# Pacing the input statistics and giving TensorE idle transposes at the start of a two-layer graph-attention and mixture-of-experts kernel

## The chip, the cores and the metric

One NeuronCore of one Trainium2 chip runs the whole program in one launch. The metric is the device time of one execution in microseconds (us), the median of several runs. Five engines work beside each other, each through its own instructions in program order: TensorE (PE; its weight loads are listed apart as PEld), VectorE (DVE), ScalarE (ACT), GpSimd (POOL) and SyncE (SP, here the queue that issues most DMAs). They wait for each other on semaphores.

## The reference, cut to what matters

The input `x` is 2708 x 256 in float32, `adj` is 2708 x 2708 in int32. Each of two layers is a graph attention followed by a top-2 mixture of experts. The change touches only the first steps of the first attention:

```python
def _layernorm(x, axis=-1, eps=1e-5):
    m = jnp.mean(x, axis=axis, keepdims=True)
    v = jnp.var(x, axis=axis, keepdims=True)
    return (x - m) / jnp.sqrt(v + eps)

def _L0_gnn_ref(x, adj, W, a):
    h = x @ W.T
    a1, a2 = (a[:F_OUT], a[F_OUT:])
    s_i = h @ a1
    s_j = h @ a2
    e = jax.nn.leaky_relu(s_i[:, None] + s_j[None, :], negative_slope=0.2)
    att = jnp.where(adj > 0, e, NEG_INF)
    att = jax.nn.softmax(att, axis=1)
    return att @ h

x = x + _L0_gnn_ref(_layernorm(x, axis=-1), adj, L0_gnn_W, L0_gnn_a)
x = x + _L0_ffn_ref((_layernorm(x, axis=-1))[None], ...)[0]
x = x + _L1_gnn_ref(_layernorm(x, axis=-1), adj, 1, L1_gnn_W_gcn, L1_gnn_W_att, L1_gnn_a_att)
x = x + _L1_ffn_ref((_layernorm(x, axis=-1))[None], ...)[0]
```

## The kernel before

The 2708 rows of `x` are held in 22 tiles: 20 of 128 rows and two of 74. The stages follow each other: the front (normalise, project and score all 22 tiles), the attention of layer 0 in 11 pairs of tiles, the experts of layer 0, the attention of layer 1, its experts. The order of instructions on PE, ACT, DVE and SP is the order in which the program writes them.

**Before the front.** SP issues the loads of `x`, of the weight `L0_gnn_W` (two 128 KB pieces), of the score vectors `a0`, of the first two tiles of `adj`, and some fills of a scratch buffer. POOL builds the 128 x 128 identity `ident`. PE then transposes the weight: four transposes into the tile `w0_ps` (L341), which ACT copies to `w0_t` (L344). `score_weights` has DVE multiply `w0_t` with `a0` (L351).

**The front loop** (from L1438) counts steps 0, 1, 2, ...; step `t` begins tile `t`. At the head of each step DVE takes the statistics of some more tiles (`read_tile`: `bn_stats` at L481 and `bn_aggr` at L482). Up to and including step `s` it has read `min(T, 2 + 2 * step)` tiles: two for each step, all 22 by step 10. The tiles are read in groups, the list `firsts`: two pairs (0, 1), (2, 3), then groups of four. When the last tile of a group is read, `deviations(group)` is started: in that step ACT computes the reciprocal deviation in two activations (`root`, L488 and L489), and one step later DVE mends it by one Newton step of three small instructions (`mend`, L391).

The rest of a step is handed out by `Turns`, a list of generators. Every entry that is due is moved one stage on, older entries first. A tile's own generator is `front(t, r)`:

- step t: DVE normalises the tile into `xn` (L497), with four buffers; POOL adds it to the running sum `x_total` (L1254);
- step t+1: PE transposes it in two halves into `tr_ps` (L515);
- step t+2: ACT copies the result to `xt` (L1259);
- step t+3: PE projects it with `w0_t` in four matmuls into `h_ps` (L520; two calls, each seen as two records);
- step t+4: ACT writes `g_all` (L1264, L1265);
- for odd t: PE spreads the scores of the pair into `e_ps` at step t+5 (L1287), and DVE copies them to `e_bc` (L1291) at step t+6.

Among these lie the masks of the first two tiles of `adj`. DVE turns a first part of the integer rows to 8-bit masks (L1316), a step later PE transposes them (`mask_turn`, L1302, into a PSUM tile with the tag `mt`, of which there are two), another step later ACT copies them away (L1308). Tile 0 has its two DVE parts in steps 9 and 12, tile 1 in steps 14 and 17. After a tile's second DVE part SP issues the load of the tile of `adj` two further on.

At step `START` = 21 the attention begins: ACT and DVE build the weights `z` of one pair of tiles against tile `j` (L1332, L1335), and four steps later PE accumulates them (`gather`, L1346, `att_ps`). After tile 21 `front_mean` closes the front: PE multiplies `x_total` (L1273), and the result goes into the last row block of `g_all`.

Of the kernel before, what the change touches and what calls it, by code (L numbers as in the profile page):

```python
# [22 lines left out]
P = 128  # L23
# [124 lines left out]
def kernel(  # L148
# [25 lines left out]
    nc = tc.nc  # L174
# [7 lines left out]
    T = TF + 2  # L182
# [3 lines left out]
    tiles = [(t, P if t < TF else TAIL) for t in range(T)]  # L186
    pairs = [tiles[k:k + 2] for k in range(0, T, 2)]
    chunks = [tiles[k:k + 4] for k in range(0, T, 4)]
    firsts = [tiles[0:2], tiles[2:4]] + chunks[1:]

    ENDS1, EARLY_ENDS1 = (6, 12, 18, T), (12, 18)
    groups1 = [tiles[a:b] for a, b in zip((0, *ENDS1), ENDS1)]
# [25 lines left out]
    def ps_tile(name, tag="wide", dtype=F32):  # L218
        return stage["pool"].tile([P, 2048 // mybir.dt.size(dtype)], dtype, name=name, tag=tag,
                                  bufs=stage["tags"][tag])  # L220
# [95 lines left out]
    ident = const.tile([P, P], F32, name="ident")  # L316
# [17 lines left out]
    def w0_tile():  # L334
        return keep0.tile([P, DC * (D + 3)], F32, name="w0_t")

    w0_t = w0_tile().rearrange("p (c d) -> p c d", c=DC)
    for c in range(DC):
        ps = ps_tile("w0_ps")
        for o in range(DC):  # L340
            nc.tensor.transpose(  # L341
                ps[:, o * P:(o + 1) * P], w0_rows[o][:, c * P:(c + 1) * P], ident
            )
        nc.scalar.copy(w0_t[:, c, :D], ps[:, :D])  # L344

    def score_weights():
        raw = a0_pool.tile([P, DC, 2], F32, name="raw")
        for c in range(DC):
            for k in range(2):
                junk = row_tile("junk", 4)  # L350
                nc.vector.scalar_tensor_tensor(  # L351
                    junk, w0_t[:, c, :D], 1.0, a0[k], op0=OP.mult, op1=OP.mult,
                    accum_out=raw[:, c, k:k + 1])
        for k, (which, coef) in enumerate(((1, 0.2), (1, 0.8), (0, 0.8))):
            nc.scalar.activation(w0_t[:, :, D + k], raw[:, :, which], AF.Copy, scale=coef)
# [205 lines left out]
    def sums_d(name, zero=False):  # L561

        t = dram.tile([W + P, D], F32, name=name)
        lo = 0 if zero else T
        nc.sync.dma_start(t[lo * P:, :].rearrange("(t p) d -> p t d", p=P),
                          nobody[:, :D].unsqueeze(1).to_broadcast([P, T + 1 - lo, D]))
        return t
# [196 lines left out]
    def parts_of(name, b2):  # L764
        E = b2.shape[0]
        whole = [xn_tile()[:, :D] for _ in range(2)]
        part = [xt_tile()[:, :P].bitcast(BF16) for _ in range(3)]
        nc.gpsimd.memset(whole[0], 0.0)
        for k in range(3):
            nc.gpsimd.dma_start(whole[0][32 * k:32 * k + E], b2)  # L770
        for k in range(3):
            a = whole[k % 2]
            nc.gpsimd.tensor_copy(part[k], a)
            if k < 2:
                nc.gpsimd.tensor_tensor(whole[1 - k % 2], a, part[k], OP.subtract)
        res = const.tile([P, D], BF16, name=name)
        for k in range(3):
            nc.gpsimd.tensor_copy(res[32 * k:32 * k + 32], part[k][32 * k:32 * k + 32])
        return res
# [16 lines left out]
    class Experts:  # L796
# [163 lines left out]
        def weigh(self, b):  # L960

            xg = self.rows[b]
            side, w = (self.pool.tile([P, 1], F32, name=nm, bufs=3) for nm in ("side", "w"))
            nc.vector.tensor_scalar(side, xg[:, D + 1:D + 2], mine_of[:, b:b + 1], -0.5,  # L964
                                    op0=OP.is_equal, op1=OP.add)
            nc.scalar.activation(w, xg[:, D + 2:D + 3], AF.Tanh, scale=side)  # L966
            return w
# [282 lines left out]
    def front(t, r):  # L1250

        xn = xn_tile()[:, :D]
        ln_a0.apply(xn[:r], x_all[:r, t, :], t, r)
        nc.gpsimd.tensor_tensor(x_total[:r], x_total[:r], xn[:r], OP.add)  # L1254
        yield 1
        ps = turn_rows(xn[:r], r)
        yield 1
        xt = xt_tile().rearrange("p (c n) -> p c n", n=P)
        nc.scalar.copy(xt[:, :, :r], ps)  # L1259
        yield 1  # L1260
        ps = ps_tile("h_ps", "acc")
        project(ps[:r, :D + 3], xt, w0_t, r)
        yield 1 if t < LAST else 2
        nc.scalar.activation(g_all[:r, t, D:], ps[:r, D:D + 3], AF.Exp)  # L1264
        nc.scalar.activation(g_all[:r, t, :D], ps[:r, :D], AF.Copy, scale=g_all[:r, t, D:D + 1])  # L1265
        if t % 2:
            yield 1
            yield from front_spread(pairs[t // 2])

    def front_mean():  # L1270
        ps = ps_tile("total_ps", "acc")[:, :DC * 96].rearrange("p (c n) -> p c n", n=96)
        for c in range(DC):
            nc.tensor.matmul(ps[:, c], x_total[:, c * P:(c + 1) * P], ones_f, start=True, stop=True)  # L1273
        total = row_tile("junk", 4)[:, :DC * 96].rearrange("p (c n) -> p c n", n=96)
        yield 1
        nc.scalar.copy(total, ps)
        yield 1
        mean = ps_tile("mean_ps", "acc")
        project(mean[:96, :D], total, w0_t[:, :, :D], 96)
        yield 1  # L1280
        nc.scalar.activation(g_all[64:96, LAST, :D], mean[64:96, :D], AF.Copy, scale=TINY / N)
# [30 lines left out]
    def mask_tile(i, r, first, turn, keep):  # L1312

        for part, (lo, hi) in enumerate(PARTS):
            cols = slice(2 * P * lo, min(2 * P * hi, N))
            nc.vector.tensor_scalar(mask_rows(i)[:r, cols], adj_rows(i)[:r, cols], 0.0, -1.0,  # L1316
                                    op0=OP.is_gt, op1=OP.mult, saturate=False)
            if part and i + 2 < T:
                load_adj(*tiles[i + 2])
            yield first  # L1320
            mask_turn(i, r, part)
            yield keep
            mask_keep(i, r, part)
            if not part:
                yield max(turn - keep - first, 0)
# [14 lines left out]
    def gather(pair, j):  # L1340
        k = rows_of(j)
        z = zs.pop((pair[0][0], j))
        for q, (i, r) in enumerate(pair):
            if j == 0:
                accs[i] = ps_tile("att_ps", "acc")
            nc.tensor.matmul(accs[i][:r, :D + 1], z[:k, q * P:q * P + r], g_all[:k, j, :D + 1],  # L1346
                             start=(j == 0), stop=(j == LAST))
# [74 lines left out]
    late, read = [], 0  # L1422

    def read_tile():

        group = next(g for g in firsts if g[0][0] <= read <= g[-1][0])
        ln_a0.stats(x_all[:group[read - group[0][0]][1], read, :], *group[read - group[0][0]])
        if read == group[-1][0]:
            turns.start(deviations(group))
# [8 lines left out]
    for step in range(START + T * len(pairs)):  # L1438
        for _ in range(fills.get(step, 0)):
            router0.fill(filled_to, filled_to + 10)  # L1440
            filled_to += 10
        while read < min(T, 2 + 2 * step):
            read_tile()
            read += 1
        if step == 0:
            turns.step()
            score_weights()
        if step < T:
            turns.start(front(*tiles[step]))
        if step == T:  # L1450
            turns.start(front_mean())
        if step == START:
            sums0 += [sums_d(f"sums0_{k}", zero=k == 1) for k in range(2)]
        if step >= START:
            k, j = divmod(step - START, T)
            weigh(pairs[k], j)
            late.append((pairs[k], j))
            if len(late) > LAG:
                gather(*late.pop(0))
            if j == LAG - 1 and k > 0:  # L1460
                turns.start(close0(pairs[k - 1], LAG, 3), 3)
            if k + 1 < len(pairs) and j in (0, 11):
                nxt = pairs[k + 1]
                if j // 11 < len(nxt):
                    turns.start(mask_tile(*nxt[j // 11], 4, 4, 3))
            if (k, j) == (2, 0):
                experts0.load_b1()
            if j == 8 and k in (1, 2):
                b2_parts.append(parts_of(f"b2_{k - 1}", (L0_ffn_b2, L1_ffn_b2)[k - 1]))
            if k == len(pairs) - 1 and j == 16:  # L1470
                assert experts0.known
                experts0.fetch(0)
                for b in range(2):
                    experts0.load(b)
                    experts0.fetch(b + 1)
        turns.step()
# [1025 lines left out]
```

## Time and profile before

| what | value |
|---|---|
| median of 3 runs | 1133.14 us (1131.94 to 1135.37) |
| the profiled execution: time | 1137.78 us |
| the profiled execution: span of its instructions | 1136.1 us |
| PE busy over the span | 1039.2 us (91%) |
| DVE busy over the span | 545.7 us (48%) |
| first normalised tile (`xn` of tile 0) begins | 9.03 us |
| first transpose of tile 0, of tile 21 (L515) | 9.59 us, 45.65 us |
| first accumulation of the attention (L1346) | 49.95 us |
| the load of `adj` tile 2 is issued; its mask is begun | 31.89 us; 44.67 us |

The profile is one execution. A busy PE is modelled to the end of its pipelined matmuls. Timeline lines give the start and the duration in us, the engine, the line of the kernel, the operation, output<-inputs, shapes and a count; a bracket gives the idle time before the instruction and what ended it. Consecutive instructions of one line are merged into one row with a count. A window line gives busy time and instruction count for each engine in a stretch, then the granted TensorE clock (1.00 is full) and the DMA share.

### The profile page before, as it was taken

How to read it: one execution, taken by the hardware profiler on the slowest of the kernel's cores; microseconds unless marked ns; L12 is line 12 of the kernel's file. 1: busy time of each engine (PE TensorE's matmuls, PEld its weight loads, DVE VectorE, ACT ScalarE, POOL GpSimd, SP SyncE). 2: the span in 40 equal slices, each digit the busy share in tenths (PEclk: the TensorE clock that was granted, in tenths of full speed). 3: DMA queues.
4: the chain of work that ended last, by engine and by line, in shares of the span. 5: the costliest groups of instructions: out<-in, count | busy, mean ns of one | idle time of the engine just before them, and what ended most of it. 6: DMA issues, size and time to landing. Idle time of an engine off the chain costs nothing. (4 is left out here: it accounts for less than half of the span.)

```text
span 1136.1 us, 21474 instructions
## 1 busy us (share of the span) xinstructions
PE 1039.2 (91%) x6707; PEld 922.6 (81%) x6707; DVE 545.7 (48%) x2210; ACT 577.9 (51%) x1602; POOL 368.7 (32%) x425
## 2 busy tenths in 40 slices
PE   5999999998989999999999999898994957999984
PEld 3888888887879999999999954898983846999873
DVE  7788888886431110011001347578775643122257
ACT  4876767665434444444444446445653522444454
POOL 7531113111242211222123271352623155443350
PEclk9999999999989999999999999999997878999998
DMA  9955444431888999999899959301215645685893
GB/s 295 313 211 174 139 175 149 172 94 36 306 256 279 324 325 319 319 325 314 257 311 366 338 156 296 133 1 56 76 39 150 163 145 129 154 208 100 227 315 110
DMA packets 161862, 234.38 MB, mean 206 GB/s; under 512 B 10891, under 2 KB 137798, under 8 KB 159032
## 3 DMA queue, kind: packets, MB, share of 16 engines
q1 hardware_dynamic: 143356, 209.90, 56.0%
q0 software_dynamic: 18384, 23.03, 10.6%
q8 instruction: 56, 0.92, 0.3%
q14 instruction: 66, 0.54, 0.1%
HBM read 205.54 MB, written 54.59 MB: 229 GB/s over the span
## 5 line engine op out<-in xcount | busy, mean ns | idle before, releaser
L996 DVE TENSOR_SCALAR yo<-out_ps,w 128x256 f32<-128x256 f32 x89 | 43.1, 484 | 384.0 <-PE out_ps L990 376.7
L1346 PE MATMUL att_ps<-g_all,z 128*128 128x257 f32 (+3 forms) x968 | 225.3, 385 | 0.0
L1346 PEld LDWEIGHTS att_ps<-g_all,z 128*128 128x128 f32 (+3 forms) x968 | 176.0, 187 | 29.9 <-issue 2.9
L990 PE MATMUL out_ps<-room,ht 128*128 128x256 f32 x840 | 192.0, 381 | 0.0
L972 PEld LDWEIGHTS hid_ps<-xt,room 128*128 128x128 f32 x1504 | 175.8, 193 | 9.6 <-issue 5.0
L972 PE MATMUL hid_ps<-xt,room 128*128 128x128 f32 x1504 | 177.8, 276 | 5.8 <-issue 2.6
L990 PEld LDWEIGHTS out_ps<-room,ht 128*128 128x128 f32 x840 | 155.9, 191 | 20.2
L1332 ACT ACTIVATE zr<-e_bc,minus_one,g_all 128x256 f32<-128x256 f32 (+3 forms) x242 | 130.5, 591 | 41.8 <-DVE z L1335 41.5
L1773 PE MATMUL att_ps<-half,wide_mask 128*128 128x258 f32 (+1 forms) x962 | 130.6, 295 | 14.2 <-issue 7.2
L976 ACT ACTIVATE ht<-hid_ps,w_t 128x128 f32<-128x128 f32 x376 | 128.7, 364 | 28.2 <-PE hid_ps L972 8.3
L1001 POOL DMA_INDIRECT sums<-yo,xg x43 | 66.8, 1554 | 226.9 <-DVE side L964 152.8
L1773 PEld LDWEIGHTS att_ps<-half,wide_mask 128*128 128x128 f32 (+1 forms) x962 | 124.5, 199 | 17.6 <-issue 13.3
L753 POOL DMA_INDIRECT rows_d<-xr,place x88 | 91.7, 1041 | 119.8 <-DVE xr L497 66.5
L1335 DVE SCALAR_TENSOR_TENSOR z<-zr,mask_t 128x256 f32<-128x256 f32 (+3 forms) x242 | 99.1, 428 | 35.1 <-ACT zr L1332 19.1
L976 ACT ACTIVATE ht<-hid_ps,w1x 128x128 f32<-128x128 f32 x180 | 65.0, 366 | 82.5 <-PE hid_ps L972 68.1
L1001 POOL DMA_INDIRECT sums<-yo,xr x42 | 65.3, 1554 | 122.9 <-DMA sums<-yo,xr 34.5
L966 ACT ACTIVATE w<-xg,side 128x1 f32<-128x1 f32 x43 | 12.7, 294 | 163.4 <-DVE side L964 159.5
L1621 POOL CAST wide_mask<-mask_t 128x1408 fp32r<-128x1408 fp8e4 x34 | 47.0, 1388 | 93.1 <-PE att_ps L1773 92.9
L515 PE MATMUL tr_ps<-ident,xr 128*128 128x128 f32 (+1 forms) x214 | 39.3, 294 | 15.3 <-ACT xr L506 13.0
L972 PE MATMUL hid_ps<-lo,wide_mask 128*128 128x128 f32 x368 | 49.5, 290 | 3.5 <-ACT lo L1108 2.9
L972 PEld LDWEIGHTS hid_ps<-lo,wide_mask 128*128 128x128 f32 x368 | 47.9, 205 | 5.7 <-ACT lo L1108 3.9
L515 PEld LDWEIGHTS tr_ps<-ident,xr 128*128 128x128 f32 (+1 forms) x214 | 27.8, 152 | 22.9 <-ACT xr L506 14.3
(334 smaller groups left out, 1450.4 us busy)
## 6 DMA issues: line engine op xcount, KB each, us to landing
room<-in_L_ffn_W_dram SPq DMA_DIRECT2D x94, 1024.0 KB
room<-in_adj_dram SPq DMA_DIRECT2D x20, 1354.0 KB
wide_mask<-in_L_ffn_w_dram SPq DMA_DIRECT2D x46, 512.0 KB
room<-in_L_ffn_w_dram SPq DMA_DIRECT2D x22, 512.0 KB
mask_t<-in_L_ffn_w_dram SPq DMA_DIRECT2D x22, 512.0 KB
rows_d<-nobody SPq DMA_DIRECT2D x1, 7511.0 KB
rows_d<-nobody SPq DMA_DIRECT2D x5, 1295.0 KB
sums<-nobody SPq DMA_DIRECT2D x2, 2944.0 KB
```

Of the source, the lines that this page charges most:

```text
L515: nc.tensor.transpose(ps[:, c, :r], src[:, c * P:(c + 1) * P], ident[:r, :r])
L753: ins = nc.gpsimd.indirect_dma_start(out=self.rows_d[:, :], in_=self.rows[t][:r], in_offset=None, out_offset=bass.IndirectOffsetOnAxis(ap= ...
L972: nc.tensor.matmul(ps[:, :P], w1_b[:, c, f * P:(f + 1) * P], xt[:, c, :], start=(c == 0), stop=(c == DC - 1))
L976: nc.scalar.activation(ht[:, f, :], ps[:, :P], self.func, bias=self.bias[:, f, b:b + 1])
L990: nc.tensor.matmul(ps[:, :D], ht[:, f, :], self.rooms[b % self.deep][1][:, f, :], start=False, stop=(f == self.FC - 1))
L996: nc.vector.tensor_scalar(yo, ps[:, :D], w, None, op0=OP.mult)
L1001: ins = nc.gpsimd.indirect_dma_start(out=self.sums[k][:, :], in_=yo, in_offset=None, out_offset=bass.IndirectOffsetOnAxis(ap=self.rows.pop ...
L1332: nc.scalar.activation(zr[:k, :n], e_bc[:k, lo:lo + n], AF.Relu, bias=minus_one[:k], scale=g_all[:k, j, D + 1:D + 2])
L1335: nc.vector.scalar_tensor_tensor(z[:k, :n], zr[:k, :n], 1.0, mask_t[:k, j // 2, lo:lo + n, j % 2], op0=OP.add, op1=OP.mult)
L1346: nc.tensor.matmul(accs[i][:r, :D + 1], z[:k, q * P:q * P + r], g_all[:k, j, :D + 1], start=(j == 0), stop=(j == LAST))
L1621: nc.gpsimd.tensor_copy(m, src)
L1773: nc.tensor.matmul(accs[i][:, :D + 2], last_masks[i][:k] if late else wide_masks[i, j % 2][:k, j // 2, :], half_k[:k, j, :], start=(j == 0 ...
```

## The change

Three edits. The groups of the statistics become four pairs for the first eight tiles (before: two pairs and one group of four). The statistics are read at a slower pace from step 4 on: by step `s` there have been `2 + 2s - max(s - 2, 0) // 2` tiles, so that steps 4, 6, 8, 10, 12 and 13 read one tile and steps 5, 7, 9 and 11 read two; the last is read in step 13. And PE transposes the identity into a PSUM tile that nobody reads, six times ahead of the transposes of the weight and six times behind them.

```diff
-    firsts = [tiles[0:2], tiles[2:4]] + chunks[1:]
+    firsts = [tiles[k:k + 2] for k in range(0, 8, 2)] + chunks[2:]
...
+    def keep_busy(n):
+
+        ps = ps_tile("busy_ps", "mt")
+        for _ in range(n):
+            nc.tensor.transpose(ps[:, :P], ident, ident)
+
     w0_t = w0_tile().rearrange("p (c d) -> p c d", c=DC)
+    keep_busy(6)
     for c in range(DC):
         ps = ps_tile("w0_ps")
         for o in range(DC):
...
         nc.scalar.copy(w0_t[:, c, :D], ps[:, :D])
+    keep_busy(6)
...
-        while read < min(T, 2 + 2 * step):
+        while read < min(T, 2 + 2 * step - max(step - 2, 0) // 2):
             read_tile()
             read += 1
```

## The prediction

> **What bounds the kernel now.** I read first the stretches of the span, to find which engine is full where; then the timeline of 0 to 50 us engine by engine, since the change ends at step 13; then who waited for whom between 4 and 32 us. The chain that ended last covers only the end of the program and says nothing of the front.
>
> Busy time by stretch (PE, PEld, DVE, ACT, POOL; then clock, DMA share, GB/s):
>
> ```profile
> 10.00:15.00 5.00, 4.20 (x13) 3.08 (x12) 4.69 (x19) 2.05 (x8) 4.78 (x30) 1.00 1.15 316
> 25.00:30.00 5.00, 3.55 (x17) 2.56 (x16) 4.80 (x18) 2.42 (x8) 1.73 (x3) 0.73 1.09 309
> 35.00:40.00 5.00, 5.00 (x38) 4.37 (x37) 3.84 (x8) 4.09 (x14) 3.96 (x6) 1.00 0.98 340
> 100.00:150.00 50.00, 50.00 (x299) 43.62 (x298) 43.60 (x160) 33.33 (x69) 11.73 (x14) 1.00 0.48 169
> ```
>
> Until 30 us DVE is full and PE has holes; from 35 us PE is full and DVE is not; in the attention PE never pauses. So a microsecond won before the first accumulation moves all that follows by a microsecond, as long as nothing later is tied to absolute time, and I find no such thing.
>
> What fills DVE is seen in one step, step 8:
>
> ```profile
> 23.24 0.42 DVE L481 BATCH_NORM_STATS2 bn<-h_all 128x6 f32<-128x256 f32 x1
> 23.69 0.18 DVE L482 BATCH_NORM_AGGREGATE mv_a<-bn 128x2 f32<-128x6 f32 x1
> 23.79 0.39 DVE L481 BATCH_NORM_STATS2 bn<-h_all 128x6 f32<-128x256 f32 x1
> 24.22 0.18 DVE L482 BATCH_NORM_AGGREGATE mv_a<-bn 128x2 f32<-128x6 f32 x1
> 24.32 0.13 DVE L391 SCALAR_TENSOR_TENSOR stat<-mv_a,rstd_a 128x4 f32<-128x4 f32 x1
> 24.48 0.16 DVE L391 SCALAR_TENSOR_TENSOR stat<-stat,rstd_a 128x4 f32<-128x4 f32 x1
> 24.68 0.16 DVE L391 SCALAR_TENSOR_TENSOR rstd_a<-stat,rstd_a 128x4 f32<-128x4 f32 x1
> 24.76 0.41 DVE L497 TENSOR_SCALAR xn<-h_all,mv_a,rstd_a 128x256 f32<-128x256 f32 x1
> ```
>
> Two statistics take 1.08 us from start to start (23.24 to 24.32), one 0.54; a mend 0.44; only the last row feeds PE in this step. The waits say the same: PE's transposes waited 4.7 us for it.
>
> ```profile
> PE tr_ps L515 <- DVE xn L497: 4.7, 4, 2.8
> ```
>
> Two more things act on the front. POOL's running sum and DVE hold each other up:
>
> ```profile
> 15.18 0.73 POOL L1254 TENSOR_TENSOR x_total<-x_total,xn 128x256 f32<-128x256 f32 x1
> 15.32 0.60 DVE L391 SCALAR_TENSOR_TENSOR stat<-mv_a,rstd_a 128x4 f32<-128x4 f32 x1
> ```
>
> The mend of 0.13 us took 0.60 and ended when POOL did (15.92 against 15.91). Statistics in the same place keep their 0.39 to 0.43. And TensorE's clock is half at two times:
>
> ```profile
> 13.71 1.94 PE L520 MATMUL h_ps<-w_t,xt 128*128 128x259 f32 x4
> ...
> 18.70 1.04 PE L520 MATMUL h_ps<-w_t,xt 128*128 128x259 f32 x4
> ...
> 28.11 1.93 PE L520 MATMUL h_ps<-w_t,xt 128*128 128x259 f32 x4
> ```
>
> The same four matmuls take 1.94 us, then 1.04, then 1.93. The granted clock reads 0.50 from 28 to 30 us, after the hole of 1.43 us in which PE waited for the first mask. Before 17 us it reads 1.00 although the durations are doubled, so there I go by the durations.
>
> **The change, part by part.** Nothing is removed but the order.
>
> *The twelve transposes.* Four cold ones in the trace (L341) come as 0.45 us for the first and 0.90 us for three, so about 0.22 us each behind the first. Six take 0.45 + 5 x 0.22 = 1.55 us. The identity is ready at 1.62 us and the weight lands at 4.50, so the first six end by 3.2 and cost nothing; the second six run from about 6.7 to 8.2, and tile 0 wants PE at 9.59. Without that cover they would cost 2 x 1.55 = 3.1 us. Nobody reads their PSUM tile; the two `mt` buffers are next wanted by PE itself, in step 10. What do they bring? At best a full clock from 9.6 to 17 us. Tiles 4 and later wait for DVE, however: the transpose of tile 4 at 18.23 begins 0.74 us after PE was free, on `xn`. A quicker PE before that gains nothing by itself; I take 0, with 0.5 us for the upper end.
>
> Here the Trainium skill, "TensorE: Matmul & The Clock Gate", Part 4 (PE-mode transpose), speaks against the edit: transposes, it says, don't count as PE activity for the clock. Part 1 asks for some 3.4 us of sustained work. By that rule the clock is as cold at 9.6 us as before and the edit is worth 0; were it wrong, DVE makes it 0 all the same. This case's rows don't decide it: PE was all but continuously busy from 11.05 us with transposes and matmuls mixed, and was warm only near 17.
>
> *One more group.* Four pairs for a pair, a pair and a four: one more root (0.30 + 0.20 us on ACT) and one more mend (0.44 us on DVE). ACT is busy 2.05 of 5 us there and covers its part; behind the new root, which waits for tile 5's statistics at 11.97, stands the copy of tile 1, now at about 12.5; PE wants it at 13.7. DVE's 0.44 is paid in full.
>
> *The pace.* No instruction fewer: 22 statistics as before, but by `xn` of tile 9 three fewer are ahead of it. All of them come back in steps 10 to 13 (1, 2, 1, 1 where there were 2, 0, 0, 0), among the masks of tile 0. I follow DVE from tile 5, with statistics 0.54 each, mend 0.45, `e_bc` 0.33, mask parts 0.85 and 0.68 (all start to start), `xn` 0.32 to the next start and 0.41 to its end. POOL's sum runs 0.72 us from 0.14 after each `xn`; a DVE operation other than statistics or `e_bc` that meets it ends behind it (mend at once, `xn` 0.15 later, as at 32.86 to 33.62 in the trace). Until 18 us I leave all as it was: step 4 saves one statistic, but its mend then meets POOL's sum at 15.2 just as it did. End of `xn`:
>
> - tile 6: 19.54 + 0.54, held by POOL, 20.64 (before 21.48)
> - tile 7: 20.55 + 1.08 + 0.33 + 0.45 + 0.41 = 22.82 (23.33)
> - tile 8: 22.73 + 0.54, held, 23.83 (25.17)
> - tile 9: 23.74 + 1.08 + 0.85 + 0.33 + 0.41 = 26.41 (27.75)
> - tile 10: 26.32 + 0.54, mend held to 27.65, + 0.41 = 28.06 (29.59)
> - tile 11: 27.97 + 1.08 + 0.33 + 0.41 = 29.79 (31.19)
> - tile 12: 29.70 + 0.54, mask held to 31.3, mend, 32.08 (32.60)
> - tile 13: 32.00 + 0.54 + 0.33 + 0.41 = 33.28 (33.62)
> - tile 14: 33.19 + 0.85, mend held to 35.2, 35.6 (35.23)
>
> The lead is 1.3 to 1.5 us at tiles 8 to 11 and is given back by tile 14, which is even 0.4 late: the statistics were deferred, not saved. But PE had not used DVE's old lead there: it transposed tile 14 at 36.90, 1.67 us after `xn`. Now it can at 35.75, 1.15 us earlier; ACT's copy of a mask part and of tile 12 (34.9) take some 0.15 of it. From then on PE is full again at 1.32 us for a tile (29.83 to 45.65, twelve tiles), DVE's lead of 1.3 us for tile 15 on suffices, and the gain of **1.0 us** stays. On SP the load of `adj` tile 2 stands behind mask part two of tile 0: 31.3 + 0.7, hardly moved from 31.89, with 12 us until its mask.
>
> Bounds: below, if every deferred statistic ends in a POOL hold, -0.9 us (the mend twice over). Above, PE alone: from tile 4 at 18.23, 17 tiles at 1.32 would put tile 21 at 40.7 for 45.65, 5.0 us. I stand near the lower of these because the DVE rows between 10 and 35 us leave only 1.3 us idle in 25.
>
> **Sum.** 1136.1 - 1.0 = 1135.1 us of span; the profiled time lies 1.7 above its span and 4.6 above the median, so the same 1.0 from the median: 1133.14 - 1.0 = **1132.1 us**, with 1131.0 to 1133.2 if this case holds.
>
> **The rivals.**
>
> 1. *Nothing is gained*: DVE's sum of work to tile 14 is the same plus 0.44, and ACT's in-order copies behind roots that now come in steps 11 and 13 eat the rest. For it: DVE 4.8 of 5 us. Against it: PE's unused lead of 1.67 us at tile 14. 1133.14 + 0.2 = 1133.3 us.
> 2. *Much is gained*: with other timings DVE's mend and `xn` of tile 4 slip between POOL's sums at 15 to 18 us (they were held 0.45 + 0.6 + 0.63 = 1.7 us), and the hole before the first mask no longer cools PE (3.4 us at half, 1.7 us of work). 1.0 + 1.7 + 1.7 = 4.4: 1128.7 us. Against it: both holds depend on tenths, and the hole stays about 1.1 to 1.4 us by my rows.
> 3. *Slower*: PE now waits for the mask's second part and the late `xn` in steps 12 to 14 and falls to half clock there. Two such stretches of 3.4 us cost 1.7 us each beside the 0.9 of the lower bound: 4.3, 1137.4 us. It decides from the point where PE's holes in 31 to 37 us reach the 1.43 that cooled it at 27. Against it: I find holes under 1 us.
>
> **How the numbers follow.** Forecast 0.52, rival 1 0.22, rival 2 0.18, rival 3 0.08. About 0.3% (3.4 us) is what a measurement of this kernel tells from no change; the three runs shown spread by as much. Faster by more takes nearly all of rival 2: 0.17. Slower by more takes most of rival 3: 0.07. The rest, 0.76, lies within. The range reaches to rival 2's edge and past rival 1: 1128.9 to 1135.2.
>
> **What would show it.** Right: `xn` of tile 9 ends near 26.4, of tile 14 near 35.6; tile 21 is transposed near 44.6 and the first accumulation begins near 48.9; four projections still take about 1.9 us at 13 us; DVE rows of L391 and L497 beside POOL's L1254 are still stretched. Wrong: the projections take 1.04 us from the start and tile 4 is transposed before 17.5 (the transposes count after all, and PE was worth more than I say), or the first accumulation moves by over 2 us either way, or it moves as I say and the attention behind it doesn't follow.

## The result, and the profile after

Twelve runs of each kernel were made beside each other. Before: median 1133.47 us (1130.48 to 1136.45). Changed: 1134.55 us (1129.45 to 1137.37). The ratio on record is 0.9998 with a 95% interval of 0.998 to 1.0016 (the two medians by themselves give 1.0010): no difference that these runs can tell, and none above some 2 us either way. The profiled execution of the changed kernel has a span of 1134.3 us, against 1136.1.

The front did become shorter, in the two profiles by twice what was predicted. In the profile of the changed kernel (timeline of PE; start, duration):

```profile
12.07 2.07 PE L528 MATMUL h_ps<-w_t,xt 128*128 128x259 f32 x4
...
17.55 0.41 PE L523 MATMUL tr_ps<-ident,xn 128*128 128x128 f32 x2 [0.21 <-DVE xn L505]
...
24.99 0.51 PE L1310 MATMUL mt_ps<-ident_bf,room 128*128 128x128 bf16 x6 [1.35 <-DVE room L1324]
...
25.55 1.04 PE L528 MATMUL h_ps<-w_t,xt 128*128 128x259 f32 x4
...
43.56 0.29 PE L523 MATMUL tr_ps<-ident,xn 74*128 74x74 f32 x2
...
47.87 1.03 PE L1354 MATMUL att_ps<-g_all,z 128*128 128x257 f32 x4
```

(Lines of the changed kernel from the edit on stand 7 or 8 further down: L523 for L515, L1354 for L1346.) The projections still begin at half clock. Tile 4 is transposed at 17.55 for 18.23, tile 21 at 43.56 for 45.65, and the attention's first accumulation begins at 47.87 for 49.95: 2.08 us earlier. By its last accumulation the lead is 1.1 us (294.7 for 295.8). The stretches that answer to those shown before:

```profile
10.00:15.00 5.00, 4.05 (x12) 2.91 (x13) 4.62 (x22) 1.84 (x8) 4.78 (x30) 1.00 1.15 317
25.00:30.00 5.00, 4.42 (x28) 3.41 (x28) 4.80 (x17) 3.30 (x11) 2.19 (x3) 1.00 1.10 269
35.00:40.00 5.00, 5.00 (x34) 4.32 (x33) 4.75 (x9) 4.50 (x15) 4.17 (x6) 1.00 1.04 309
100.00:150.00 50.00, 50.00 (x298) 43.71 (x295) 42.84 (x158) 34.43 (x71) 12.59 (x15) 1.00 0.47 162
```

From 25 to 30 us PE does more (4.42 for 3.55) at a full clock. DVE is as full as before there, and from 35 to 40 us it is fuller, 4.75 for 3.84: the deferred work has moved. The attention is unchanged.

What is new stands between 50 and 80 us (timeline, DVE's masks and PE's use of the last):

```profile
57.90 0.99 DVE L1324 TENSOR_SCALAR room<-room 128x1536 fp8e4<-128x1536 int32 x1 [3.82 <-DMA room<-in_adj_dram]
...
69.34 0.96 DVE L1324 TENSOR_SCALAR room<-room 128x1536 fp8e4<-128x1536 int32 x1 [4.04 <-DMA room<-in_adj_dram]
...
70.36 0.51 PE L1310 MATMUL mt_ps<-ident_bf,room 128*128 128x128 bf16 x6 [0.71 <-DVE room L1324]
```

DVE waits for the loads of `adj` tiles 3 and 4, 7.9 us together (0.4 before), and PE stops for the second, for 0.71 us. That is one place where the lead goes. The next sections ask how much of the lead each edit makes, where it is given back, and why the total doesn't show it.

### The profile page after: what moved, and what is told of

Same layout as the page of the kernel before. It is cut to its first block, busy times and chain, and to the rows that moved or that the text cites. A ratio compares the mean times of both kernels' runs of the same rounds, so it can differ in the third digit from the quotient of the medians.

```text
span 1134.3 us, 21500 instructions
## 1 busy us (share of the span) xinstructions
PE 1045.1 (92%) x6719; PEld 927.5 (82%) x6719; DVE 541.2 (48%) x2213; ACT 577.6 (51%) x1604; POOL 366.3 (32%) x425
## 5 line engine op out<-in xcount | busy, mean ns | idle before, releaser
L1354 PE MATMUL att_ps<-g_all,z 128*128 128x257 f32 (+3 forms) x968 | 225.4, 385 | 0.0
L1354 PEld LDWEIGHTS att_ps<-g_all,z 128*128 128x128 f32 (+3 forms) x968 | 175.9, 187 | 29.8 <-issue 2.9
L1340 ACT ACTIVATE zr<-e_bc,minus_one,g_all 128x256 f32<-128x256 f32 (+3 forms) x242 | 130.2, 591 | 46.2 <-DVE z L1343 45.9
L1781 PE MATMUL att_ps<-half,wide_mask 128*128 128x258 f32 (+1 forms) x962 | 134.0, 299 | 14.5 <-issue 6.9
L1781 PEld LDWEIGHTS att_ps<-half,wide_mask 128*128 128x128 f32 (+1 forms) x962 | 127.3, 202 | 18.4 <-issue 14.0
L1343 DVE SCALAR_TENSOR_TENSOR z<-zr,mask_t 128x256 f32<-128x256 f32 (+3 forms) x242 | 96.0, 416 | 31.9 <-ACT zr L1340 18.7
L523 PE MATMUL tr_ps<-ident,xr 128*128 128x128 f32 (+1 forms) x214 | 39.7, 297 | 14.8 <-ACT xr L514 13.0
L523 PEld LDWEIGHTS tr_ps<-ident,xr 128*128 128x128 f32 (+1 forms) x214 | 28.1, 153 | 22.6 <-ACT xr L514 14.3
```

The costliest lines, as they stand in the source:

```text
L523: nc.tensor.transpose(ps[:, c, :r], src[:, c * P:(c + 1) * P], ident[:r, :r])
L1340: nc.scalar.activation(zr[:k, :n], e_bc[:k, lo:lo + n], AF.Relu, bias=minus_one[:k], scale=g_all[:k, j, D + 1:D + 2])
L1343: nc.vector.scalar_tensor_tensor(z[:k, :n], zr[:k, :n], 1.0, mask_t[:k, j // 2, lo:lo + n, j % 2], op0=OP.add, op1=OP.mult)
L1781: nc.tensor.matmul(accs[i][:, :D + 2], last_masks[i][:k] if late else wide_masks[i, j % 2][:k, j // 2, :], half_k[:k, j, :], start=(j == 0 ...
```

## The experiments

Totals differ between chips: `before_again`, `after_again`, `stats_only` and `busy_only` were made where the kernel before takes 1102 us, `pace_only`, `pairs_only`, `busy_24t` and `busy_12m` where it takes 1134, the last four of the table where it takes 1138. Each has one profile. So runs are compared by marks in their own profiles: when PE begins the first and the last accumulation of layer 0's attention (L1346 in the numbering before), how long DVE waited there for `adj` (47 to 110 us), and whether TensorE's clock fell once between 250 and 270 us. "Between" is the difference of the two marks.

| run | first | last | between | DVE for adj | clock fall |
|---|---|---|---|---|---|
| before | 49.95 | 295.8 | 245.8 | 0.4 | yes |
| before_again | 49.21 | 293.4 | 244.2 | 0.9 | no |
| busy_only | 49.76 | 295.6 | 245.9 | 1.1 | yes |
| pairs_only | 48.63 | 292.8 | 244.2 | 5.4 | no |
| pace_only | 47.84 | 293.9 | 246.1 | 7.4 | yes |
| stats_only | 47.79 | 293.7 | 245.9 | 1.9 | yes |
| changed kernel | 47.87 | 294.7 | 246.8 | 7.9 | yes |
| after_again | 47.85 | 293.7 | 245.9 | 4.3 | yes |
| busy_24t | 47.82 | 294.9 | 247.1 | 7.8 | yes |
| busy_12m | 47.73 | 292.9 | 245.1 | 7.9 | no |
| after_zero_late | 47.82 | 293.4 | 245.6 | 2.2 | yes |
| after_fills_late | 48.73 | 294.5 | 245.8 | none | yes |
| after_nosum | 46.71 | 294.2 | 247.5 | 8.5 | yes |
| before_nosum | 46.95 | 293.4 | 246.5 | 5.1 | yes |

**Both kernels once more**, unchanged.

> The kernel before, unchanged, once more. If the front is set by DVE's order, the first accumulation of the attention begins again near 49.95 us (within 0.3) and the attention's last accumulation near 295.8. If the clock's phase sets it, it moves by 0.5 us or more, with the time at which the four projections fall from 1.9 to 1.04 us. The total may differ by several us, through the second layer.

> The changed kernel, unchanged, once more. DVE's order: first accumulation again near 47.9 us, last one near 294.7, with DVE waiting for adj's load at about 58 and 69 us as in the first profile. If the wait for adj was chance, it is gone and the last accumulation is near 293.7.

The changed kernel repeats to 0.02 us on another chip. The kernel before does not: 49.21, 0.74 us earlier. In the two profiles `xn` of tiles 2 to 18 ends within 0.04 us, so DVE didn't make the difference; PE's rows part at 27 us, over the clock. In the second profile PE isn't cooled by the hole before the first mask. Its projection there (timeline of PE, before_again):

```profile
27.71 1.04 PE L520 MATMUL h_ps<-w_t,xt 128*128 128x259 f32 x4
```

took 1.93 us in the first. So 0.74 of the first pair's 2.08 us is this fall of the clock in one execution, and **1.36 us** (49.21 - 47.85) is the change, by this one uncooled run of the old order. The hole itself is nearly as long in the changed kernel, 1.35 us for 1.43, and didn't cool PE in its runs. DVE's wait for `adj` was shorter in the repeat, 4.3 us, and PE didn't stop: the give-back differs from run to run.

**The two parts apart**: `stats_only` is the changed kernel without `keep_busy` (first diff), `busy_only` the changed kernel with the old statistics (second).

```diff
-    keep_busy(6)
...
-    keep_busy(6)
```

```diff
-    firsts = [tiles[k:k + 2] for k in range(0, 8, 2)] + chunks[2:]
+    firsts = [tiles[0:2], tiles[2:4]] + chunks[1:]
...
-        while read < min(T, 2 + 2 * step - max(step - 2, 0) // 2):
+        while read < min(T, 2 + 2 * step):
```

> The pairs and the slower pace without the twelve transposes. If the transposes bring nothing (my theory): first accumulation within 0.3 us of the changed kernel's 47.9. If they warm the clock and that counts (rival): the projections stay at 1.9 us up to about 17 us or longer, and the first accumulation is 0.5 us or more later, 48.4 and above.

> The twelve transposes alone, statistics as before the change. My theory: first accumulation near 49.95 us, as before. Rival (they warm the clock): it is earlier by 0.5 us or more, and the projections reach 1.04 us before 16 us.

47.79 without the transposes, 49.76 with them alone: the statistics make the gain and the twelve transposes nothing. The rival falls on both. (49.76 is later than 49.21 although PE wasn't cooled here either: the first tile was normalised late, its `xn` ending at 10.37 us for 9.60 in `before_again`. By this run the gain would be 1.9 us; so 1.36 is good to about half a microsecond.)

**Pace and pairs apart**, neither with the transposes; both start from the kernel before.

```diff
-        while read < min(T, 2 + 2 * step):
+        while read < min(T, 2 + 2 * step - max(step - 2, 0) // 2):
```

```diff
-    firsts = [tiles[0:2], tiles[2:4]] + chunks[1:]
+    firsts = [tiles[k:k + 2] for k in range(0, 8, 2)] + chunks[2:]
```

> The slower pace, with tiles 4 to 7 still one group and without the transposes. In the changed kernel the mend of the pair (6, 7) no longer met POOL's running sum and tile 4 was normalised 0.7 us earlier. If the pace is what brings the gain, the first accumulation is within 0.4 us of 47.9. If the pairs are needed (the root of a group of four waits for tile 7 and delays tile 4), it is between 48.5 and 49.95.

> The four pairs at the old pace, without the transposes: one root and one mend more and nothing deferred. If the pace brings the gain: no gain, 49.95 us or up to 0.5 later. If the pairs bring it by themselves: 48.9 us or earlier.

The pace alone gives all of it, 47.84. The pairs alone came to 48.63, within what was said for pairs that bring a gain by themselves; against the uncooled 49.21 that is 0.6 us. Tile 4's `xn` ends at 17.28 there, at 18.08 before, so DVE got past one POOL sum sooner. Together the two give no more than the pace.

**More work for TensorE at the start**: 24 transposes, or 12 plain products.

```diff
-    keep_busy(6)
+    keep_busy(12)
...
-    keep_busy(6)
+    keep_busy(12)
```

```diff
-            nc.tensor.transpose(ps[:, :P], ident, ident)
+            nc.tensor.matmul(ps[:, :P], ident, ident, start=True, stop=True)
```

> The changed kernel with two times twelve transposes for two times six, so that TensorE has work all but without a gap from 1.7 to 9.4 us. If transposes count for the clock, the first projections (12 us) take 1.04 us and not 2.0. If they do not, they take 1.9 to 2.0 us as with twelve. The first accumulation is near 47.9 us either way if DVE sets it; 47.4 or earlier if the cold clock still costs something.

> The changed kernel with two times six plain float32 products of the identity with itself for the transposes; each should take about twice a transpose's time, so that TensorE is busy about as long as with 24 transposes. If plain products count for the clock where transposes do not, the first projections take 1.04 us here and 1.9 to 2.0 there. If both runs agree, the kind of instruction is not what matters. First accumulation near 47.9 us if DVE sets it.

PE was busy for the same time in both ahead of the first tile (timeline of PE; first busy_24t, then busy_12m):

```profile
6.59 2.77 PE L341 MATMUL busy_ps<-ident 128*128 128x128 f32 x12
9.87 0.61 PE L523 MATMUL tr_ps<-ident,xn 128*128 128x128 f32 x2 [0.51 <-DVE xn L505]
11.29 0.42 PE L523 MATMUL tr_ps<-ident,xn 128*128 128x128 f32 x2 [0.82 <-DVE xn L505]
11.68 1.14 PE L528 MATMUL h_ps<-w_t,xt 128*128 128x259 f32 x4
13.29 0.41 PE L523 MATMUL tr_ps<-ident,xn 128*128 128x128 f32 x2 [0.47 <-DVE xn L505]
13.54 1.04 PE L528 MATMUL h_ps<-w_t,xt 128*128 128x259 f32 x4
```

```profile
6.60 2.77 PE L341 MATMUL busy_ps<-ident 128*128 128x128 f32 x12
9.61 0.66 PE L523 MATMUL tr_ps<-ident,xn 128*128 128x128 f32 x2 [0.24 <-DVE xn L505]
11.05 0.66 PE L523 MATMUL tr_ps<-ident,xn 128*128 128x128 f32 x2 [0.77 <-DVE xn L505]
11.50 2.02 PE L528 MATMUL h_ps<-w_t,xt 128*128 128x259 f32 x4
...
13.73 1.47 PE L528 MATMUL h_ps<-w_t,xt 128*128 128x259 f32 x4
```

With 24 transposes PE is warm from about 10 us (its clock record begins at full speed at 10.29); in the other runs the projections come down between about 14.4 and 17. With 12 products, recorded as twice 12 matmuls, it is cold at 11 (the first projections took 2.02 and 1.47 us). One run of each doesn't settle whether the kind of work or the clock's phase makes that difference. The phase is the likelier, though not shown: in each profile all changes of the clock lie whole multiples of 3.41 us apart, and counted back that way the burst from 6.59 us falls into one such stretch in `busy_24t` (6.87 to 10.29) all but for 0.3 us, and is split between two in `busy_12m` (at 7.78). The runs do settle two things: nothing but transposes had run on PE when its clock came up in `busy_24t`, so transposes can warm it, and a warm clock at the start is worth nothing here (47.82 against 47.87). DVE sets the pace.

**POOL's running sum left out**, in both kernels.

```diff
-        nc.gpsimd.tensor_tensor(x_total[:r], x_total[:r], xn[:r], OP.add)
```

> The changed kernel without POOL's running sum of the normalised tiles (it leaves out the mean row of layer 0, which stays zero). If POOL's sum holds DVE's mend and normalise rows and so pins tile 4 to 17.4 us whatever stands ahead of it, the front is 1 to 2.5 us shorter: first accumulation at 45.5 to 46.9 us, and no mend or normalise row is stretched. If the stretch costs nothing because PE or ACT bound the front, it stays at 47.0 or above (0.7 us at least go with the wait for the sum at the end).

> The kernel before without POOL's running sum (the same part left out). If my hold accounting is right, the old order loses more through the sum at tile 4 than the new one: first accumulation 2 to 3 us earlier than its 49.2 to 49.95. If the holds fall equally on both orders, the difference between this run and the one before it is again 1.4 us.

Tile 4 in the changed kernel (timeline of DVE and POOL):

```profile
15.17 0.79 POOL L1262 TENSOR_TENSOR x_total<-x_total,xn 128x256 f32<-128x256 f32 x1
...
15.84 0.13 DVE L399 SCALAR_TENSOR_TENSOR stat<-mv_a,rstd_a 128x2 f32<-128x2 f32 x1
...
16.23 0.74 POOL L1262 TENSOR_TENSOR x_total<-x_total,xn 128x256 f32<-128x256 f32 x1
16.29 1.11 DVE L505 TENSOR_SCALAR xn<-h_all,mv_a,rstd_a 128x256 f32<-128x256 f32 x1
```

and without the sum (after_nosum, timeline of DVE):

```profile
15.26 0.13 DVE L399 SCALAR_TENSOR_TENSOR stat<-mv_a,rstd_a 128x2 f32<-128x2 f32 x1
...
15.70 0.41 DVE L505 TENSOR_SCALAR xn<-h_all,mv_a,rstd_a 128x256 f32<-128x256 f32 x1
```

1.11 us against 0.41: the stretching of this row is the sum's doing. It fits this that the new order's front ends at 47.73 to 47.87 in seven runs although tile 0 was transposed anywhere from 9.61 to 10.25 us: POOL's first sum begins near 15.15 in all of them, behind POOL's own preparations, and DVE falls in step with it. Without the sum, tile 21 is transposed at 41.34 (new order) and 43.52 (old), 2.2 us apart. Some 0.5 of that is a later start (tile 0 was transposed at 9.75 and 10.24); about 1.7 us, an estimate, is the order. With the sum it was 1.35 (43.56 against 44.91). So most of the new order's lead doesn't hang on the holds: it is there without any. Whether the sum costs the old order more at tile 4, as was supposed, the two unequal starts leave open.

Yet the first accumulation comes at 46.71 and 46.95, only 0.24 apart, for in the new order DVE now stands before the load of `adj` tile 2 (after_nosum, timeline of DVE and PE):

```profile
42.83 0.96 DVE L1323 TENSOR_SCALAR room<-room 128x1536 fp8e4<-128x1536 int32 x1 [2.39 <-DMA room<-in_adj_dram]
...
44.94 1.07 PE L528 MATMUL h_ps<-w_t,xt 128*74 128x259 f32 x4 [1.75 <-DVE e_bc L1298]
```

The mask blocks DVE's queue, `e_bc` is behind it, and PE waits for that. A faster front runs into `adj`'s supply. It also means that the 46.95 and 46.71, though both within the ranges named, don't confirm what the ranges were worked out from.

**Giving `adj` the queue.** `after_zero_late` moves a 2.9 MB zero fill (first diff); `after_fills_late` has that and moves the last three fills of `rows_d`, first one and then two, behind the loads of `adj` tiles 2 and 3 (second).

```diff
-            sums0 += [sums_d(f"sums0_{k}", zero=k == 1) for k in range(2)]
+            sums0.append(sums_d("sums0_0"))
+        if step == START + 4 * T:
+            sums0.append(sums_d("sums0_1", zero=True))
```

```diff
-    fills = {0: 2, 11: 1, 16: 2}
+    fills = {0: 2, 13: 1, 18: 2}
```

> The changed kernel with one 2.9 MB zero fill (the second half of sums0, read only by the experts) issued in the attention's fifth pair instead of at its start, so that it does not stand ahead of adj's later tiles. If the queue ahead of adj is what gives part of the front's gain back, DVE waits for adj at most 4 us in all (7.4 to 7.9 in three of the four runs of this kind) and PE not at all, and the attention takes 244.2 us from first to last accumulation, or 245.9 when the clock falls once at 250 to 270 us. If the give-back is chance or the writing itself, it stays at 245.1 or 246.8.

> The same, and the last two fills of rows_d are moved behind the loads of adj tiles 2 and 3 (steps 13 and 18 for 11 and 16). My theory: no wait of DVE for adj above 1 us, first accumulation near 47.8 us, the attention 244.2 us (245.9 with a clock fall). In the total some 2 us less than the kernel before, which the spread of the runs (1129 to 1137) may hide. If something else than adj holds the attention up, no difference to the run before this one.

In the first, the wait for tile 4 is gone, 2.2 us for tile 3 remain and PE never stops (between: 245.6 with a clock fall). In the second no wait for `adj` is left (245.8 with a fall). What SP issued, and for how long (timeline of SP; first the changed kernel, then after_fills_late):

```profile
30.83 9.03 SPq L605 DMA_DIRECT2D rows_d<-nobody  x2
39.95 4.23 SPq L289 DMA_DIRECT2D room<-in_adj_dram  x1
```

```profile
38.05 0.35 SPq L289 DMA_DIRECT2D room<-in_adj_dram  x1
38.45 6.80 SPq L605 DMA_DIRECT2D rows_d<-nobody  x2
```

The load of tile 3 took SP until 44.18 us behind the fills and until 38.40 ahead of them; its mask began at 57.90, after a wait, and at 56.49 without one. So it was what stood ahead in the queue, as far as one profile of each can say: the waits differ between runs of one kernel too (7.9 and 4.3). The first accumulation of `after_fills_late` came late, at 48.73: in that execution the score vectors landed at 8.19 us (7.84 in the changed kernel's profile), DVE was that much later and tile 3 met the first POOL sum:

```profile
15.11 1.19 DVE L505 TENSOR_SCALAR xn<-h_all,mv_a,rstd_a 128x256 f32<-128x256 f32 x1
```

In time, `after_fills_late` had a median of 1134.39 us (12 runs) beside 1138.25 for the kernel before (17 runs): ratio 0.9971, interval 0.9948 to 0.9994, some 0.3% shorter. The changed kernel was not run beside it, so how much of that is due to the fills isn't shown.

## Why the prediction was right or wrong

**The total**: 1132.1 with 1128.9 to 1135.2 and no measurable change as likeliest; measured 1134.55, ratio 0.9998. The time lies in the range and no change could be told. That says little for the working: a gain of 1 us couldn't have been told from none, and two steps that failed pull in opposite directions, a front gain that was larger than predicted and a lead that didn't all reach the end. Two of the signs that it named for being wrong came: the first accumulation moved by over 2 us in the pair of profiles (2.08), and the attention behind it didn't follow it all the way.

**The twelve transposes at nothing**: right, by `busy_only` and `stats_only`, and for the reason given: even a warm clock from 10 us on (`busy_24t`) moves nothing. The Trainium skill says in "TensorE: Matmul & The Clock Gate", Part 4 (PE-mode transpose), that full speed doesn't engage for transposes, since they don't count as busy time in the same way. One profile here shows otherwise: 24 of them, in two bursts of 2.8 us, and the clock was full some 4 us earlier than in any other run.

**The pace, "until 18 us I leave all as it was"**: the failed term. I had the mend of step 4 meet POOL's sum at 15.2 as before. It began at 15.84, in that sum's last tenth of a microsecond, and ran at 0.13 us. Tile 5's `xn` ended at 18.94, where I had 19.62, and tile 6 wasn't held. From tile 6 on my list is late by a steady 0.8 to 1.0 us: tile 9 at 25.58 (26.41 predicted), tile 11 at 28.91 (29.79), tile 14 at 34.60 (35.6). The steps after it were sized well, the mask's hold among them (1.03 us, PE waits 1.00 for it). The upper rival named this slip and priced it at 1.7; it was 0.7 to 1.0.

**The gain at the first accumulation**: 1.0 predicted; 1.36 between runs that weren't cooled, 2.08 in the pair of profiles, of which 0.74 is the kernel before at half clock from 27.3 to 30.7 us. That 1.0 came near 1.36 is luck. PE's unused lead at tile 14, which I read as 1.67 us, was 0.95 without the cooling (36.16 against 35.21 in `before_again`), so it was 0.7 too large, and my list of `xn` was 1.0 late there: two errors that nearly cancel. The rival's 1.7 for the cooling was too high: the two profiles of the kernel before are 0.74 apart.

**"A microsecond won before the first accumulation moves all that follows"**: wrong. I looked for later work tied to absolute time and found none, and checked only `adj` tile 2 on SP. The DMA engines were full from 10 to 50 us (shares of 0.98 to 1.15 in the stretches shown, 1.05 to 1.10 in each ten us of the changed kernel), so the landing of tiles 3 and 4 was tied to the bytes ahead of them. By the table: the attention takes 244.2 us where PE doesn't wait for a mask and the clock doesn't fall, and 245.6 to 245.9, mostly about 245.85, with a fall and no such wait, so a fall costs 1.4 to 1.65. The changed kernel's 246.8 hold 0.95 more, `busy_24t` 1.2, `busy_12m` (no fall) 0.9, `pace_only` 0.2; `stats_only` and `after_again` on the other chip nothing; `before_nosum` 0.65 and `after_nosum`, with the earliest front, 1.65. PE's own waits for the masks in these six runs are 0.2 to 1.15 us and make most of it. So of 1.36 us between nothing and 1.2 is returned 20 us later.

**What hides the rest** is the clock, in the second layer above all. In the twelve runs of the changed kernel the time follows the granted clock: the three below 1131 us have 0.963 or 0.964 as its mean, the other nine 0.955 to 0.960. Each hole of PE there may or may not cool it. One difference between the two profiles, in work that keeps PE full, follows a hole of 4.4 us near 770 us that is there in every run (the changed kernel's stretches behind it; PE, PEld, DVE, ACT, POOL; clock, DMA share, GB/s):

```profile
775.00:779.00 4.00, 3.28 (x15) 3.08 (x16) 3.69 (x16) 3.02 (x8) 0.00 (x0) 0.50 0.39 131
779.00:783.00 4.00, 4.00 (x22) 4.00 (x20) 1.33 (x10) 2.99 (x7) 0.00 (x0) 0.50 0.02 4
783.00:787.00 4.00, 4.00 (x20) 4.00 (x21) 2.17 (x11) 1.00 (x1) 0.00 (x0) 0.50 0.00 0
787.00:791.00 4.00, 4.00 (x33) 4.00 (x33) 1.61 (x4) 3.06 (x10) 1.36 (x1) 0.94 0.35 104
```

and in the kernel before, behind the same hole:

```profile
778.00:782.00 4.00, 3.26 (x17) 3.06 (x18) 3.69 (x16) 3.09 (x9) 0.00 (x0) 0.57 0.39 133
782.00:786.00 4.00, 4.00 (x37) 4.00 (x36) 3.23 (x20) 3.23 (x8) 0.00 (x0) 1.00 0.02 4
```

Half clock for 13.65 us here, for 3.41 there. At half the work that is 5.1 us, more than the whole gain. The changed kernel was 3.0 us ahead at the end of this hole (775.72 against 778.74) and 1.8 us at the end of the span. It was the short stretch in `before`, `before_again` and `busy_only`, and the long one in the other eleven: three of five profiles with the old pace, none of nine with the new. Whether the change alters the odds of it or this is chance stays open: nothing was tried on it. Nor is it all: from 20 to 1095 us the two profiles were at half clock for 77.9 us (before) and 85.3. Were every run of the changed kernel long and every run before short, the medians should lie some 4 us apart (5.1 less 1.36, and more with the return), and the interval (2.3 us down, 1.8 up) says they don't.

## What to carry to other kernels

Deferring work on a full engine pays by the lead that the next engine left unused; read that lead from more than one profile, for part of it here was a fall of the clock. Count the holds of two engines on each other instruction by instruction: in `after_fills_late` the first tile was transposed 0.13 us later than in `pace_only` (10.38 for 10.25), the sum held a tile sooner, and the front ended 0.9 later. When a front gets shorter, look at every transfer that its consumers will want earlier, not only the next one, and ask which bytes stand ahead in the queue. For a gain of 0.1 to 0.2% compare marks inside profiles and repeat them: here seven of eight fronts of the new order with the sum agree to 0.14 us, where the totals spread over 8.

## What was not expected of the hardware

TensorE stayed at half clock for 13.65 us, four times 3.41, although its rows show it busy for the last 8 of them without a hole (4.00 of 4.00 twice). In another run the same work behind the same hole had its full clock back after 3.41 us. And one chip ran the same program in 1102 us, others in 1134 to 1138; its half-clock time between 20 and 1095 us was 45.9 us in `before_again`, for 77.9 in `before`, which at half the work accounts for 16 of the 42 us between these two executions.
